# Attention scores in one float32r pass over stacked halves, maxima by pairs of rounds, weights four rounds behind

## The chip, the cores and the metric

The kernel runs on one core of a Trainium2 chip. The core has five engines that work side by side, each through its own list of instructions in order: PE (matrix products, with weight loads of its own shown as PEld), DVE (vector), ACT (activation functions), POOL (a second vector engine) and SP, which here only issues transfers (DMAs). PE writes to PSUM, a small memory of eight banks; the others read PSUM and the working memory, POOL the working memory only. The metric is the time on the device in microseconds (us); less is better.

## What is computed

Two layers. Each has a normalisation with a learned shift and scale, an attention and a feed-forward part. Only the attention of the first layer bears on the change: 16 batches of 256 tokens, 128 wide, 16 heads of 8.

```
qkv = x @ Wqkv + bqkv                  # q, k, v: 16 heads of 8
content = einsum('bhid,bhjd->bhij', q, k)
rel = einsum('bhid,rd->bhir', q, rel_emb)      # shifted by one, cut to 256
scores = (content + rel) / sqrt(8)
out = einsum('bhij,bhjd->bhid', softmax(scores), v) @ Wout + bout
```

`rel` is added to k beforehand, so that one product gives content and rel together. After that come a mixture of 16 experts (four chosen per token), then the second layer. All data are 32-bit floats.

## The kernel before

The work goes by chunks of two batches (8 chunks) and, in the attention of the first layer, by rounds: a round `n` is a batch `b` and a quarter `r` of its heads, so four heads, and there are 64 rounds, 8 per chunk. The 128 partitions hold four groups `g` of 32 rows. The main loop (over `n`, line 727 on) writes the order of every engine by hand; the scheduler keeps it. In each turn it issues:

- `scores(n)`: eight matmuls of 32 rows by 256 columns, two for each of four heads, each head in its own PSUM bank (`s`, L441). The operands are `qx` and `kx`: a head's 8 rows of q (others are zero, by the mask `of_head`), and k with a row of ones (row 16 of each group).
- `row_maxima` (L453): DVE takes the maximum over each row of `s`, negated. `with_maxima` (L461 to L465): DVE transposes the maxima, and SP writes them by four small DMAs into row 16 of `qx`, opposite the ones of k, so that the next product has the maximum subtracted.
- `weights(n - LAG)` with LAG = 2: the same product turned round, keys in rows (`st`, L475), and ACT's exp of it (L483).
- `values(n - LAG - 1)` (L495): the product with v, which ACT copies out (L506, L509) and POOL adds (L510).
- steps of other tasks, generators that stop at places ("dve", "mid", "end", "take", "after", "late"), of which one step per place is taken in a round: `project` (normalisation of the next chunk, `pq`, `pk`, `pv`: L568, L576, L590), `attn_end` (division, output product, gate), `chunk_end` (second normalisation, router logits, router).
- one of `later_loads`: DMAs of inputs that are needed later.

`projected` makes the operands: for each of NU = 2 halves of the heads it takes `pq` and `pk`, ACT writes `qx` from `pq` twice (L571), and DVE writes `kx` from `pk`, with the bias and `rel` added (L578). All PSUM tiles of the stage come from one pool of eight banks, `pa_m`; a bank goes to the next tile when the last reader of its old tile is through, and that next tile's first matmul waits for it. At the start ACT loads its table (L163) and applies tanh to the conditioning input (L163, `silu`); `project_first` then does chunk 0 batch by batch (L608 on).

Of the kernel before, what the change touches and what calls it, by code (L numbers as in the profile page):

```python
# [15 lines left out]
ENG = mybir.EngineType  # L16
IN_ORDER = {ENG.PE, ENG.DVE, ENG.Activation, ENG.Pool}

# [11 lines left out]
ONES = 16  # L30
# [26 lines left out]
def tile_adaln_two_layers(ctx: ExitStack, tc: tile.TileContext, a: dict, out: bass.AP):  # L57
# [53 lines left out]
    wq = load("wq", [P, NU, P], a["wq"])  # L111
    wk = load("wk", [P, NU, P], a["wk"])
    wv = load("wv", [P, P], a["wv"])
    bq = load("bq", [P, NR], a["bq"])
    of_head = load("of_head", [P, NS], a["of_head"])
    bk = load("bk", [P, NU], a["bk"])
# [147 lines left out]
    with ExitStack() as moe_scope:  # L264
# [87 lines left out]
        with ExitStack() as scope:  # L352
            ap = scope.enter_context(tc.tile_pool(name="attn", bufs=2))
            ap1 = scope.enter_context(tc.tile_pool(name="attn1", bufs=1))
            rt = scope.enter_context(tc.tile_pool(name="route", bufs=2))
# [14 lines left out]
            maxima = [ap1.tile([P, NIT, 32], F32, tag=f"maxima{i}", name=f"maxima{i}") for i in range(3)]  # L370

# [17 lines left out]
            for t in maxima:  # L389
                nc.gpsimd.memset(t, 0.0)  # L390
            filled(0, nc.vector)
# [38 lines left out]
            LAG = 2  # L430
# [3 lines left out]
            def scores(n):  # L434
# [3 lines left out]
                for i in range(NIT):  # L438
                    for g in range(4):
                        rows_ = slice(32 * g, 32 * g + 32)  # L440
                        nc.tensor.matmul(  # L441
                            s[g][:, i, :],
                            qs[c][r][rows_, k, ts(i, P)],
                            ks[c][rows_, r // NS, k, :],
                            start=True,
                            stop=True,
                        )
                return s

            def row_maxima(n, s):  # L450
                mx = maxima[n % 3]
                for g in range(4):
                    nc.vector.tensor_reduce(mx[:, :, g], s[g], AX.X, ALU.max, negate=True)  # L453
                return mx

            def with_maxima(n, mx):

                b, r = rounds[n]
                c, k = divmod(b, 2)
                turned = ap.tile([P, NIT, 32], F32, tag="turned", name=f"turned_{n}", bufs=3)  # L460
                nc.vector.transpose(turned.rearrange("p i t -> p (i t)"), mx.rearrange("p i t -> p (i t)"))  # L461
                row = qs[c][r].rearrange("(g x) k t -> x g k t", x=32)[ONES, :, k, :]
                row = row.rearrange("g (i m t) -> m g i t", i=NIT, m=4)
                for m in range(4):
                    nc.sync.dma_start(row[m], turned[32 * m : 32 * m + 4])  # L465

            def weights(n):
# [3 lines left out]
                st = [bank([P, NIT, T], f"st_{n}_{g}") for g in range(4)]  # L471
                for i in range(NIT):
                    for g in range(4):
# [3 lines left out]
                            ks[c][rows_, r // NS, k, ts(i, P)],  # L477
                            qs[c][r][rows_, k, :],
                            start=True,
                            stop=True,  # L480
# [73 lines left out]
            def operands(c):  # L554
                qs[c] = {r: ap.tile([P, 2, T], F32, tag=f"qx{r}", name=f"qx_{c}_{r}") for r in range(NR)}
                ks[c] = ap.tile([P, NU, 2, T], F32, tag="kx", name=f"kx_{c}")

            def projected(c, hT, of):
# [4 lines left out]
                for u in range(NU):  # L563
                    yield "mid"
                    if u == 0 and c:
                        operands(c)
                    pq = bank([P, n, T], f"pq_{at}_{u}")
                    nc.tensor.matmul(pq, wq[:, u, :], h2, start=True, stop=True)  # L568
                    for s in range(NS):
                        r = NS * u + s  # L570
                        nc.scalar.activation(  # L571
                            qs[c][r][:, of, :], pq, AF.Identity, bias=bq[:, r : r + 1], scale=of_head[:, s : s + 1]
                        )
                    yield "end"
                    pk = bank([P, n, T], f"pk_{at}_{u}")
                    nc.tensor.matmul(pk, wk[:, u, :], h2, start=True, stop=True)  # L576
                    yield "take"
                    nc.vector.scalar_tensor_tensor(  # L578
                        ks[c][:, u, of, :],
                        pk,  # L580
                        bk[:, u : u + 1],
                        rel.unsqueeze(1).to_broadcast([P, n, T]),
                        ALU.add,
                        ALU.add,
                    )
# [7 lines left out]
            def project(c):  # L593
# [4 lines left out]
                hT = ap.tile([P, 2, T], F32, tag="hT", name=f"hT_{c}")  # L598
# [113 lines left out]
            hT_first = ap.tile([P, 2, T], F32, tag="hT", name="hT_0")  # L712
# [13 lines left out]
            next_chunks = {max(LAG, 2 * NR * c): c + 1 for c in range(NCH - 1)}  # L726
            for n in range(len(rounds) + LAG + 1):
                if n < len(rounds):
# [5 lines left out]
                    with_maxima(n, row_maxima(n, s))  # L734
# [9 lines left out]
                take_step("end")  # L744
                take_step("take", True)
# [15 lines left out]
                if n == 40:  # L761

                    nc.gpsimd.tensor_scalar(b_gu[:, 0, :], b_gu[:, 0, :], ALPHA, None, ALU.mult)
                    nc.gpsimd.tensor_scalar(b_gu[:, 1, :], b_gu[:, 1, :], 1.0, None, ALU.add)
            take_step("take", True)

# [810 lines left out]
def _layout(inputs):  # L1577
# [6 lines left out]
    def at_heads(v):  # L1584

        o = np.zeros(v.shape[:-1] + (NU, 4, 32), f)
        v = v.reshape(v.shape[:-1] + (NU, NS, 4, DH))
# [74 lines left out]
```

## Time and profile before

| what | value |
| --- | --- |
| median of 3 runs | 1073.02 us (1072.72 to 1073.31) |
| the profiled run's own time | 1072.42 us |
| its span, first to last instruction | 1070.3 us |
| mean granted clock of PE | 0.993 |
| instructions | 15978 |
| first and last `s` of the attention rounds | 11.6 and 290 us |
| first matmul of the experts (L813) | 302.7 us |

A row of the page's groups names the line, the engine, the operation and the tiles (out<-in), how often it ran, its busy time, the mean duration in ns, and the idle time of its engine just before it with what ended that idle time. In the timelines the first two numbers are start and duration in us, x4 says that four instructions of one kind are merged into a row, and the bracket names the idle time of that engine before it and who ended it. In the table by stages each engine has its busy time and number of instructions, then come the clock of PE, the busy share of the DMA engines and GB/s. "SPq" rows are the issues of DMAs by SP.

### The profile page before, as it was taken

How to read it: one execution, taken by the hardware profiler on the slowest of the kernel's cores; microseconds unless marked ns; L12 is line 12 of the kernel's file. 1: busy time of each engine (PE TensorE's matmuls, PEld its weight loads, DVE VectorE, ACT ScalarE, POOL GpSimd, SP SyncE). 2: the span in 40 equal slices, each digit the busy share in tenths (PEclk: the TensorE clock that was granted, in tenths of full speed). 3: DMA queues.
4: the chain of work that ended last, by engine and by line, in shares of the span. 5: the costliest groups of instructions: out<-in, count | busy, mean ns of one | idle time of the engine just before them, and what ended most of it. 6: DMA issues, size and time to landing. Idle time of an engine off the chain costs nothing. (4 is left out here: it accounts for less than half of the span.)

```text
span 1070.3 us, 15978 instructions
## 1 busy us (share of the span) xinstructions
PE 1019.3 (95%) x5333; PEld 520.1 (49%) x5333; DVE 833.5 (78%) x1285; ACT 718.4 (67%) x1515; POOL 796.5 (74%) x756
## 2 busy tenths in 40 slices
PE   7999999999999999999999999898999999999987
PEld 5566666666654444444444434333444444444334
DVE  6678878998834466766656566899999999999995
ACT  3676677667666777687767756365676767767662
POOL 3245434543457678887888788899999999999992
PEclk8999999999999999999999999999999999999999
DMA  4102100000052222322222222100001000000000
GB/s 118 42 11 61 53 13 2 3 4 2 4 179 81 98 99 80 118 105 94 109 90 90 89 95 102 59 10 10 21 0 30 15 15 30 1 10 6 5 11 20
DMA packets 35537, 53.14 MB, mean 50 GB/s; under 512 B 8416, under 2 KB 23296, under 8 KB 35456
## 3 DMA queue, kind: packets, MB, share of 16 engines
q1 hardware_dynamic: 34912, 51.87, 14.5%
q8 instruction: 42, 0.69, 0.3%
q14 instruction: 39, 0.32, 0.1%
q10 hardware_dynamic: 544, 0.26, 0.1%
HBM read 46.34 MB, written 5.51 MB: 48 GB/s over the span
## 5 line engine op out<-in xcount | busy, mean ns | idle before, releaser
L483 ACT ACTIVATE exp<-st 128x512 f32<-128x512 f32 x256 | 132.2, 602 | 87.6 <-PE st L475 87.6
L453 DVE TENSOR_REDUCE maxima<-s 128x2 f32<-128x512 f32 x256 | 158.8, 683 | 26.2 <-PE s L441 26.0
L828 POOL TENSOR_TENSOR u<-u,wide 128x512 f32<-128x512 f32 x128 | 163.0, 1273 | 10.3 <-DVE u L827 0.2
L827 DVE SCALAR_TENSOR_TENSOR u<-pg,u 128x512 f32<-128x512 f32 x128 | 87.7, 686 | 78.8 <-POOL u L821 78.8
L836 PE MATMUL acc<-u,w_dn 128*128 128x512 f32 x256 | 134.0, 605 | 6.4 <-POOL u L828 6.2
L1241 DVE TENSOR_TENSOR_SCAN sum_assoc<-keep,bound_assoc 128x1024 f32<-128x1024 bf16 (+1 forms) x58 | 125.7, 2168 | 9.6 <-POOL bound_assoc L1238 9.6
L813 PE MATMUL pg<-hT,w_gu 128*128 128x512 f32 x256 | 131.2, 594 | 0.4 <-DVE logits L675 0.4
L815 PE MATMUL pup<-hT,w_gu 128*128 128x512 f32 x256 | 130.8, 593 | 0.6 <-ACT u L818 0.6
L821 POOL TENSOR_SCALAR u<-u 128x512 f32<-128x512 f32 x128 | 79.6, 622 | 62.8 <-ACT u L818 56.5
L1238 POOL TENSOR_TENSOR bound_assoc<-v,phasor 128x1024 f32<-128x1024 f32 x57 | 124.6, 2185 | 1.6 <-ACT phasor L1224 1.6
L1459 POOL TENSOR_TENSOR sum_assoc<-sum_assoc,phasor 128x1024 f32<-128x1024 f32 (+1 forms) x58 | 121.3, 2091 | 0.4 <-DVE sum_assoc L1241 0.3
L816 ACT ACTIVATE pg<-pg,b_gu 128x512 f32<-128x512 f32 x128 | 84.0, 656 | 52.6 <-PE pg L813 52.0
L1241 DVE TENSOR_TENSOR_SCAN mem<-keep,bound_pos 128x1024 f32<-128x1024 bf16 x52 | 118.1, 2271 | 0.0
L1238 POOL TENSOR_TENSOR bound_pos<-v,rotor 128x1024 f32<-128x1024 f32 x51 | 111.4, 2185 | 0.0
L1255 PE MATMUL pout<-m_pos,w_pos 128*128 128x512 f32 x204 | 97.2, 599 | 14.2 <-ACT oT L1280 10.8
L1255 PE MATMUL pout<-sum_assoc,w_assoc 128*128 128x512 f32 x228 | 107.6, 594 | 2.0 <-POOL sum_assoc L1459 2.0
L818 ACT ACTIVATE u<-pup,b_gu 128x512 f32<-128x512 f32 x128 | 87.8, 686 | 18.4 <-PE pup L815 16.4
L475 PE MATMUL st<-qx,kx 32*128 32x256 f32 x1024 | 82.6, 390 | 0.7 <-DMA qx<-turned 0.5
L836 PEld LDWEIGHTS acc<-u,w_dn 128*128 128x128 f32 x256 | 46.8, 190 | 73.9 <-issue 38.9
L441 PE MATMUL s<-kx,qx 32*128 32x256 f32 x1024 | 78.2, 407 | 4.1 <-DVE kx L578 1.8
L1222 ACT ACTIVATE phasor<-off 128x512 f32<-128x512 f32 x56 | 35.1, 627 | 69.6 <-DVE off L1216 64.2
L815 PEld LDWEIGHTS pup<-hT,w_gu 128*128 128x128 f32 x256 | 50.2, 196 | 60.5 <-issue 51.6
(302 smaller groups left out, 1866.8 us busy)
## 6 DMA issues: line engine op xcount, KB each, us to landing
wide<-scores SPq DMA_DIRECT2D x64, 512.0 KB
qx<-turned SPq DMA_DIRECT2D x256, 1.0 KB
there<-total SPq DMA_DIRECT2D x12, 256.0 KB
fetched<-there SPq DMA_DIRECT2D x12, 256.0 KB
w_gu<-in_gate_up_dram SPq DMA_DIRECT2D x8, 256.0 KB
out_dram<-x SPq DMA_DIRECT2D x16, 128.0 KB
x<-in_x_dram SPq DMA_DIRECT2D x14, 128.0 KB
w_dn<-in_down_dram SPq DMA_DIRECT2D x4, 256.0 KB
```

The source lines that it names most:

```text
L453: nc.vector.tensor_reduce(mx[:, :, g], s[g], AX.X, ALU.max, negate=True)
L483: nc.scalar.activation(e[:, g, :, :], st[g], AF.Exp, scale=QSCALE)
L813: nc.tensor.matmul(pg, w_gu[:, e, 0 : 2 * D : 2], h2, start=True, stop=True)
L815: nc.tensor.matmul(pu, w_gu[:, e, 1 : 2 * D : 2], h2, start=True, stop=True)
L818: nc.scalar.activation(u, pu, AF.Identity, bias=b_gu[:, 1, e : e + 1])
L827: nc.vector.scalar_tensor_tensor(u, pg, MOST, u, ALU.min, ALU.mult)
L828: nc.gpsimd.tensor_tensor(u, u, wide[n // SOME][:, n % SOME, :], ALU.mult)
L836: nc.tensor.matmul(accs[c], w_dn[:, e, :], work.pop(n), start=False, stop=(e == NE - 1))
L1238: nc.gpsimd.tensor_tensor(w[nm], v2, bind, ALU.mult)
L1241: nc.vector.tensor_tensor_scan(dst[:, half].rearrange("p s k t -> p (s k t)"), keep.rearrange("p (s k) t -> p s k t", k=2)[:, half].rearra ...
L1255: nc.tensor.matmul(pos[c], w[:, j, :], m[:, k, :, :].rearrange("p k t -> p (k t)"), start=(j == 0 and i == 0 and k == 0), stop=(c < NCH - ...
L1459: nc.gpsimd.tensor_tensor(m[:, part], m[:, part], phasor[(n - 1) % 3][:, part, :, 1:], ALU.mult)
```

## The change

- q and k are projected once each (128 rows, 16 heads of 8), not twice, and split in an upper half (the upper 20 bits, by an `and` on DVE) and the exact rest (a subtraction on POOL; for the k of chunk 0 on DVE). Both halves of both are stored to DRAM, each row twice, and read back by round, so that the 32 rows of a group hold the 8 rows of a head four times: upper and lower of q against upper and lower of k. The matmuls of `s` and `st` then run on type float32r.
- The stores and reads are queued in `copies` and issued 2 or 3 (6 before round 8) per round by SP; those of chunk 0 are issued at once, q's by ACT.
- The negated maxima of two rounds go into one tile `raw`, are split in the same way into 16 columns of `maxima`, are transposed once for two rounds, and go to 16 rows of a tile of their own, `max_rows`, by four DMAs. `with_maxima` of a pair stands behind the first reduction of the next even round.
- `weights` starts with four new matmuls of 512 columns (`takes` against `max_rows`), which add the maxima of the round to `st`. `takes` is made at the start by ACT from the input `of_round`.
- LAG is 4. The task that projects chunk 1 starts at round 1. The tiles of hT and of the router have one buffer less.

The diff, cut to its core:

```diff
-    wq = load("wq", [P, NU, P], a["wq"])
-    wk = load("wk", [P, NU, P], a["wk"])
+    wq = load("wq", [P, P], a["wq"])
+    wk = load("wk", [P, P], a["wk"])
...
-    bq = load("bq", [P, NR], a["bq"])
-    of_head = load("of_head", [P, NS], a["of_head"])
+    bq = load("bq", [P, 1], a["bq"])
+    of_round = load("of_round", [P, 2], a["of_round"])
...
+            for t in max_rows:
+                nc.gpsimd.memset(t.bitcast(F32), 0.0)
+            for i in range(2):
+                nc.scalar.activation(takes[:, i, :], ident, AF.Identity, bias=of_round[:, i : i + 1], scale=0.0)
             filled(0, nc.vector)
             sc0 = silu(0, cT0, setup)
...
-            LAG = 2
+            LAG = 4
...
-                            qs[c][r][rows_, k, ts(i, P)],
-                            ks[c][rows_, r // NS, k, :],
+                            qs[c][rows_, r, k, ts(i, P)],
+                            ks[c][rows_, r, k, :],
...
+            def upper(out, src):
+                nc.vector.tensor_scalar(out.bitcast(I32), src.bitcast(I32), UPPER_HALF, None, ALU.bitwise_and)
...
             def row_maxima(n, s):
-                mx = maxima[n % 3]
+                if n % 2 == 0:
+                    raws[n // 2] = small.tile([P, NIT, 4, 2], F32, tag="raw", name=f"raw_{n // 2}")
+                raw = raws[n // 2]
                 for g in range(4):
-                    nc.vector.tensor_reduce(mx[:, :, g], s[g], AX.X, ALU.max, negate=True)
+                    nc.vector.tensor_reduce(raw[:, :, g, n % 2], s[g], AX.X, ALU.max, negate=True)
+                    if g == 0 and n >= 2 and n % 2 == 0:
+                        with_maxima(n // 2 - 1)
+                if n % 2:
+                    mx = maxima[n // 2 % 3][:, :, 0:16].rearrange("p i (g h x) -> h p i g x", g=4, h=2)
+                    upper(mx[0], raw)
+                    nc.gpsimd.tensor_tensor(mx[1], raw, mx[0], ALU.subtract)
...
+                rows_ = max_rows[pair % 3].bitcast(F32).rearrange("(q x) (i m t) -> x m q i t", x=8, i=NIT, m=4)[0]
                 for m in range(4):
-                    nc.sync.dma_start(row[m], turned[32 * m : 32 * m + 4])
+                    nc.sync.dma_start(rows_[m], turned[32 * m : 32 * m + 16])
...
             def weights(n):
...
+                for g in range(4):
+                    rows_ = slice(32 * g, 32 * g + 32)
+                    nc.tensor.matmul(
+                        st[g],
+                        takes[rows_, n % 2, :],
+                        max_rows[n // 2 % 3][rows_, :].unsqueeze(1).to_broadcast([32, NIT, T]),
+                        start=True,
+                        stop=False,
+                    )
...
+            def halves(of_q, whole, engine):
...
+                upper(high, whole)
+                engine.tensor_tensor(whole, whole, high, ALU.subtract)
+                return high, whole
+
+            def put_aside(at, of_q, parts):
...
+                there = dram.tile([P, 4, n, T], F32, tag=f"{nm}_halves{n}", name=f"{nm}_halves_{at}")
+                to = there.rearrange("p (y z) k t -> z p y (k t)" if of_q else "p (y z) k t -> y p z (k t)", y=2)
+                return there, [
+                    (to[i], parts[i].rearrange("p k t -> p (k t)").unsqueeze(1).to_broadcast([P, 2, n * T]))
+                    for i in range(2)
+                ]
+
+            def spread(c, of, of_q, there, r, queue=nc.sync):
+
+                dst = (qs if of_q else ks)[c].bitcast(F32)[:, r, of, :]
+                queue.dma_start(dst, there[32 * r : 32 * r + 32].rearrange("n x k t -> (n x) k t"))
...
             def projected(c, hT, of):
...
+                pq = bank([P, n, T], f"pq_{at}")
+                nc.tensor.matmul(pq, wq, h2, start=True, stop=True)
+                qf = ap1.tile([P, 2, T], F32, tag="q_whole", name=f"q_whole_{at}")[:, 0:n, :]
+                nc.scalar.activation(qf, pq, AF.Identity, bias=bq)
+                q = halves(True, qf, nc.gpsimd)
+                yield "end"
+                pk = bank([P, n, T], f"pk_{at}")
+                nc.tensor.matmul(pk, wk, h2, start=True, stop=True)
+                yield "take"
...
+                k = halves(False, kf, nc.gpsimd if c else nc.vector)
+                both = []
+                for of_q, parts in ((True, q), (False, k)):
+                    queue = nc.scalar if of_q and not c else nc.sync
+                    there, moves = put_aside(at, of_q, parts)
+                    both.append((of_q, there, queue))
+                    copies.extend((lambda move=move, queue=queue: queue.dma_start(*move)) for move in moves)
+                copies.extend(
+                    (lambda r=r, each=each: spread(c, of, *each[:2], r, each[2])) for r in range(NR) for each in both
+                )
+                if not c:
+                    while copies:
+                        copies.pop(0)()
...
-            next_chunks = {max(LAG, 2 * NR * c): c + 1 for c in range(NCH - 1)}
+            next_chunks = {max(1, 2 * NR * c): c + 1 for c in range(NCH - 1)}
...
-                    with_maxima(n, row_maxima(n, s))
+                    row_maxima(n, s)
+                elif n == len(rounds):
+                    with_maxima(n // 2 - 1)
...
                 take_step("end")
+                for i in range(2 + n % 2 if n >= 2 * NR else 6):
+                    if copies:
+                        copies.pop(0)()
                 take_step("take", True)
```

## The prediction, made before the changed kernel ran

> **What bounds the kernel now.** I read the page first, then the DVE and PE timelines of the attention stage. All times are us.
>
> ```profile
> PE 1019.3 (95%) x5333; PEld 520.1 (49%) x5333; DVE 833.5 (78%) x1285; ACT 718.4 (67%) x1515; POOL 796.5 (74%) x756
> L453 DVE TENSOR_REDUCE maxima<-s 128x2 f32<-128x512 f32 x256 | 158.8, 683 | 26.2 <-PE s L441 26.0
> L475 PE MATMUL st<-qx,kx 32*128 32x256 f32 x1024 | 82.6, 390 | 0.7 <-DMA qx<-turned 0.5
> L441 PE MATMUL s<-kx,qx 32*128 32x256 f32 x1024 | 78.2, 407 | 4.1 <-DVE kx L578 1.8
> ```
>
> The change lies in the 64 rounds of attention. `s` (L441) and `st` (L475) run from 11.6 to about 298; what follows, 302.7 to the end, keeps its code, so it shifts as a whole. PE is busy almost always there, but a share of busy time does not say who waits for whom. The timelines do:
>
> ```profile
> 96.07 0.24 DVE L461 STREAM_TRANSPOSE turned<-maxima 128x64 f32<-128x64 f32 x1
> 96.86 2.48 DVE L453 TENSOR_REDUCE maxima<-s 128x2 f32<-128x512 f32 x4 [0.54 <-PE s L441]
> 101.20 2.48 DVE L453 TENSOR_REDUCE maxima<-s 128x2 f32<-128x512 f32 x4
> 289.56 1.15 PE L441 MATMUL s<-kx,qx 32*128 32x256 f32 x16
> 290.72 2.49 DVE L453 TENSOR_REDUCE maxima<-s 128x2 f32<-128x512 f32 x4 [0.75 <-PE s L441]
> ```
>
> The round at 96.86 has nothing on DVE but four reductions and a transposition: DVE idled 0.54 before it, PE sets the pace. The round at 101.20 followed two statistics, a reciprocal and a product on DVE and shows no idle: DVE sets the pace. So both engines are near their limit. Rounds take 3.3 to 5.2; from `s` of round 8 (49.1) to `s` of round 63 (289.56) they take 240.4, mean 4.37. DVE is busy some 203 of these (from the table by stages). **A faster PE can win at most what DVE leaves idle, about 37.**
>
> **PE, part by part.** A f32 matmul leaves two records (1024 records, 512 matmuls each for `s` and `st`); 16 records of `s` take 1.15, the last one 0.374 of it, so they follow at 52 ns. If a float32r matmul leaves one, `s` has 8 (0.42) and `st` 8 plus 4 new ones for the maxima (0.62), where each has 16 (0.83). From the start of `s` to DVE's first reduction it is 1.16 now (289.56 to 290.72); 8 records fewer take off 0.42, a record of half the passes some 0.1 (512 columns last 0.592, 256 last 0.374: 0.22 for 256 columns in two passes): 0.65 to 0.7. One `pq` and one `pk` per chunk go, 0.86 each (two records of 0.43). No row shows float32r: the ends are one record, as above, and two as now, with `s` to DVE at 1.16; I take one, the nearest row halved, since the diff asks for one pass.
> The Trainium skill, "TensorE: Matmul & The Clock Gate", section "LDWEIGHTS (loading the stationary operand)", says that a weight load costs its columns over 1.2 GHz, 32 rows or 128, so 107 ns here; by it the 12 loads of `st` would take 1.28, longer than now, PE would gain nothing, and the sum would be near the third rival's. This trace differs: 16 loads of `st`, each 0.185 long, pass in 0.85, so they follow at 44 ns; the measurement decides.
>
> **DVE, part by part.** Per chunk (8 rounds) it loses 4 of 8 transpositions (0.245 each) and one `kx` (0.75). It gains two masks of 128x512 (`q_high`, `k_high`) and four of 128x16. A mask of 128x512 from SBUF has no row; 128x256 (L1566) takes 0.34, the two-step 128x512 (L896) 0.84; I take 0.6. The small ones: 0.15 (128x16, L149 to L151, 0.16 to 0.28). Lost 1.7, gained 1.8: DVE's sum stays 29.4 per chunk, 32 x 0.62 of it reductions. POOL's new differences (1.27 each, row L828) lie beside reductions.
>
> A round is then 2.48 of reductions, 0.24 in even rounds, and the larger of DVE's other work and the hand-over: the banks of `s` free with the last reduction of the round before, so 0.7. The built order gives DVE's other work for a middle chunk: y and statistics 1.25; mask, statistics, inv, heads 1.75; none; mask, statistics, y 1.4; statistics and q/k halves, where `q_high` waits for ACT (four exp 2.06, po copy 0.40, q 0.80 behind one another) 3.4; mask, inv, heads 0.95; none; logits. Rounds: 3.95, 4.2, 3.4, 3.85, 6.1, 3.4, 3.4, 3.25: **31.55 per chunk**, against 33.5 (84.61 to 118.12) and later 35.2, the router's steps included. Those add 12 of DVE work, some 8.5 of it not hidden in light rounds. The last chunk has no q/k and no statistics for a next one (-3.9). Rounds 8 to 63: 7 x 31.55 - 3.25 (up to the `s` of 63) - 3.9 + 8.5 = 222.2, a gain of 18.2, **if the operands are there**.
>
> At nothing I cost: the transposition's new wait for POOL's small difference (0.2 to 0.7; it starts a reduction and a hand-over, 1.3, earlier; behind it on DVE three reductions; uncovered 0.5 every second round, 14); one buffer for hT and the router's tiles (readers were eight rounds, or one instruction of the same engine, ahead; uncovered 0.4 each); three q evictions fewer on ACT (0.8 each), which is not the limit.
>
> **The operands go through memory.** q and k halves are stored (512 KB each) and read back by round (256 KB). Prices: a 256 KB read issued alone at 903.92:
>
> ```profile
> 904.50:905.00 0.50, 0.50 (x2) 0.19 (x1) 0.50 (x1) 0.08 (x1) 0.50 (x1) 1.00 0.14 45
> 905.00:905.50 0.50, 0.50 (x3) 0.25 (x2) 0.50 (x2) 0.00 (x0) 0.50 (x1) 1.00 0.85 295
> 905.50:906.00 0.50, 0.50 (x3) 0.26 (x2) 0.50 (x2) 0.00 (x0) 0.50 (x1) 1.00 0.48 180
> 906.00:906.50 0.50, 0.50 (x3) 0.25 (x2) 0.50 (x2) 0.33 (x1) 0.50 (x2) 1.00 0.01 4
> 293.55 2.31 SPq L465 DMA_DIRECT2D qx<-turned  x4
> ```
>
> It lands 2.1 after its issue at some 320 GB/s; 512 KB so takes 2.85. Four small ones take SP 2.3.
> In SP's order the second store of k stands behind the four transfers of maxima of round 6 of the chunk, which wait for the transposition after that round's first reduction (1.6 after its `s`). Then: maxima issued by 3.9, store lands 6.65, first read of k (SP waits for the store) lands 8.6 to 9.0. `s` of the next chunk wants it after two rounds, 6.65. **PE stands 2.0 to 2.4, six times: 13.5**, and DVE with it; queued behind that `s` are all weights and values. What bounds it: nothing (if it lands in time) and 4 each (if reads of w_gu come between).
> The Trainium skill, "DMA: Bandwidth & Descriptors", section "Anatomy of one DMA — SWDGE (gpsimd) path", fits DMAs that GpSimd issues by 2.0 plus bytes over 436 GB/s: 2.6 and 3.2 for these two. By it a trip would be 0.85 longer, and the sum 5 longer; the trace has 2.1 for 256 KB from SP, and I keep that.
> Rounds 8 to 63 so take 222.2 + 13.5 = 235.7: a gain of 4.7.
>
> **The start.**
>
> ```profile
> 1.75 1.28 ACT L163 ACT_TABLE_LOAD   x1 [1.75 <-issue]
> 3.46 0.29 DVE L608 BATCH_NORM_STATS2 stats_a<-x 128x6 f32<-128x128 f32 x1
> 4.01 0.44 SPq L71 DMA_DIRECT2D of_head<-in_of_head_dram  x1
> 11.56 1.15 PE L441 MATMUL s<-kx,qx 32*128 32x256 f32 x16
> ```
>
> ACT's table load and silu now stand behind two `takes`, which wait for `of_round`, in of_head's place on SP (4.01), behind transfers that keep the DMA engines full until 5.5: about 6.1. Then 1.28, two takes 0.6, silu 0.2, DVE 0.3: DVE's statistics begin at 8.5, not 3.46, and all to `pq` moves by **5.0**. Then, where `s` followed `kx`: q (0.56), mask, difference, store of 256 KB, read of 128 KB; 1 MB of stores passes at 320 GB/s, so k's last lands near 20, its read near 22. `s` of round 0 at 22.0: **+10.4** in all.
> Rounds 0 to 3 carry no weights and are short, but batch 1 needs its own trip: 18.4 to round 4, now 19.1 (30.70 - 11.56): -0.7. Chunk 1's four stores (2 MB, 6.4) go out together after round 6's maxima; its first read of k lands about 13.5 after `s` of round 6, where 6.7 was wanted: rounds 4 to 8 take 24.1, now 18.4: **+5.7**. At round 8 the kernel is 15.4 late.
>
> **The end.** Four rounds of weights behind instead of two: two more rounds with neither `s` nor DVE work, each bound by exp and PE's `st`, `po` in turn. Now such a round is 3.05 (po at 294.99, 298.04); st is 0.2 shorter: **+5.7**.
>
> **Sum.** 15.4 - 4.7 + 5.7 = +16.4. The profiled run took 1072.4 (span 1070.3 and 2.1 around it; the median of the runs shown is 1073.0, 0.6 more): 1088.8, so 1089.0.
>
> **Rivals.**
> 1. The trip through memory is short (store and read together about 3, not 5). For: DMA is nearly idle in this stage (share 0.02 to 0.16 between 100 and 250), and the read is mostly a fixed wait. Then the six stands go (-13.5), chunk 1's shrinks by 4, the two first trips by 2 each: 1067.5, faster. It decides from 2.1 less per trip on, nine trips making up 17 to 19. Against: 256 KB alone took 2.1, and a store must land before its read is issued. Chance 0.2 for ending faster.
> 2. The trip is longer: stores slower than reads, maxima queued behind 512 KB, each stand 4: 1089 + 11 = 1100, with slower first trips 1104. Chance 0.15.
> 3. float32r does not do what it says (two records per matmul): hand-over 1.2, four light rounds per chunk lose 0.5: 1089 + 14 = 1103. Chance 0.07.
> 4. The trip is in time in the middle but not at the start: 1075, about the same. Chance 0.08.
>
> **The numbers.** My case (1080 to 1098) has 0.5. 0.2% (2 us) is about what a measurement of this kernel can tell from no change. Faster 0.2, same 0.05, slower 0.75. The range from 1068 to 1104 takes in rivals 1 and 2 for the most part.
>
> **What will show it.** Right: first `s` near 22; `s` and `st` with 512 and 768 records; DVE waits of 2 or more before the first reduction of each chunk from the second on; rounds 26 and 30 of a chunk near 3.4; MoE start near 319. Wrong: `s` of round 16, 24 and so on right behind the round before; stage end before 303; a hand-over under 0.5; a DVE mask over 0.8.

## The result and the profile after

The changed kernel takes 1117.17 us (four runs, 1116.04 to 1117.6); the kernel before, on the same chip, 1073.07. The ratio is 1.041 (95% interval 1.0397 to 1.0424). Predicted were 1089 and, as range, 1068 to 1104. The direction was right; the loss is 44, not 16.4, and the time lies outside the range.

From the page of the changed kernel: the line of the engines, then the groups of `s`, of its reduction and of ACT's exp.

```profile
PE 987.4 (89%) x4529; PEld 482.2 (43%) x4529; DVE 836.2 (75%) x1296; ACT 703.6 (63%) x1490; POOL 823.9 (74%) x807
L468 DVE TENSOR_REDUCE raw<-s 128x2 f32<-128x512 f32 x256 | 160.4, 677 | 57.7 <-PE s L448 57.5
L448 PE MATMUL s<-kx,qx 32*128 32x256 f32 x512 | 43.2, 381 | 52.1 <-DMA kx<-k_halves 39.8
```

`s` has 512 records where it had 1024: float32r leaves one record per matmul. But PE, busy nearly all the time before, now idles 52 ahead of `s` (below, a stand is such a time in which PE waits for an operand), 40 of it until a read of `kx` lands, and DVE idles 57.5 for `s`, where it was 26.

The table gives the span in five stretches, with borders read from the timelines (first reduction of a round on DVE, first expert matmul on PE). "Predicted" is the profile before plus the prediction's terms. Two experiments are shown beside it.

| stretch | before | predicted | after | `early` | `spaced` |
| --- | --- | --- | --- | --- | --- |
| to round 0 | 12.8 | 23.2 | 24.2 | 24.5 | 21.7 |
| rounds 0 to 8 | 37.5 | 42.5 | 49.5 | 50.0 | 34.2 |
| rounds 8 to 63 | 240.5 | 235.8 | 254.4 | 227.9 | 226.8 |
| round 63 to the experts | 12.0 | 17.7 | 17.3 | 17.6 | 18.5 |
| experts to the end | 767.6 | 767.6 | 770.2 | 767.3 | 768.2 |
| span | 1070.3 | 1086.8 | 1115.5 | 1087.4 | 1069.4 |

So 28.7 were missed: 18.6 in rounds 8 to 63, 7 in rounds 0 to 8, 2.6 after the stage and 1 ahead of it, less 0.4 at its end. Rounds 8 to 63 are where the gain was to be, and there the kernel loses 14.

What a chunk's border looks like, from the timeline of the changed kernel between 101 and 113 (start, duration, engine; SPq is SP issuing transfers; rows of other work left out):

```profile
101.55 0.23 DVE L479 STREAM_TRANSPOSE turned<-maxima 128x64 f32<-128x64 f32 x1
101.84 2.57 SPq L484 DMA_DIRECT2D max_rows<-turned  x4
...
104.51 0.53 SPq L638 DMA_DIRECT2D k_halves<-k_whole  x1
105.14 0.41 SPq L609 DMA_DIRECT2D qx<-q_halves  x1
105.60 0.84 SPq L272 DMA_DIRECT2D w_gu<-in_gate_up_dram  x1
...
107.83 0.32 SPq L609 DMA_DIRECT2D kx<-k_halves  x1
...
111.27 0.80 PE L448 MATMUL s<-kx,qx 32*128 32x256 f32 x8 [4.38 <-DMA kx<-k_halves]
```

This is the chain the prediction described, one link after the other (below, a trip is a store to memory and the read back). The maxima of rounds 12 and 13 are turned in round 14; their four transfers occupy SP until 104.41; only then k's second store goes out. SP waits for its landing (3.3) before it issues the read at 107.83, and that needs 3.4. PE had nothing to do from 106.9.

The landing times are in the page's part on transfers (KB each, median us from issue to landing):

```profile
qx<-q_halves SPq DMA_DIRECT2D x28, 256.0 KB, 3.2
kx<-k_halves SPq DMA_DIRECT2D x28, 256.0 KB, 3.6
q_halves<-q_whole SPq DMA_DIRECT2D x7, 512.0 KB, 3.2
k_halves<-k_high SPq DMA_DIRECT2D x7, 512.0 KB, 4.0
k_halves<-k_whole SPq DMA_DIRECT2D x7, 512.0 KB, 3.2
```

The last row is k's second store. The prediction had 2.1 for a read and 2.85 for a store.

### The profile page after: what moved, and what is told of

Read it like the earlier page. It is cut to its first block, busy times and chain, and to the rows that moved or that the text cites. A ratio compares the mean times of both kernels' runs of the same rounds, so it can differ in the third digit from the quotient of the medians.

```text
span 1115.5 us, 14249 instructions
## 1 busy us (share of the span) xinstructions
PE 987.4 (89%) x4529; PEld 482.2 (43%) x4529; DVE 836.2 (75%) x1296; ACT 703.6 (63%) x1490; POOL 823.9 (74%) x807
## 5 line engine op out<-in xcount | busy, mean ns | idle before, releaser
L468 DVE TENSOR_REDUCE raw<-s 128x2 f32<-128x512 f32 x256 | 160.4, 677 | 57.7 <-PE s L448 57.5
L1321 PE MATMUL pout<-m_pos,w_pos 128*128 128x512 f32 x204 | 99.7, 612 | 12.5 <-ACT oT L1346 9.9
L884 ACT ACTIVATE u<-pup,b_gu 128x512 f32<-128x512 f32 x128 | 87.8, 686 | 18.2 <-PE pup L881 16.2
L448 PE MATMUL s<-kx,qx 32*128 32x256 f32 x512 | 43.2, 381 | 52.1 <-DMA kx<-k_halves 39.8
L523 PE MATMUL po<-exp,v_aug 128*32 128x256 f32 x1024 | 79.9, 432 | 9.2 <-DVE raw L468 9.0
```

Source lines behind the costliest of these rows:

```text
L468: nc.vector.tensor_reduce(raw[:, :, g, n % 2], s[g], AX.X, ALU.max, negate=True)
L884: nc.scalar.activation(u, pu, AF.Identity, bias=b_gu[:, 1, e : e + 1])
L1321: nc.tensor.matmul(pos[c], w[:, j, :], m[:, k, :, :].rearrange("p k t -> p (k t)"), start=(j == 0 and i == 0 and k == 0), stop=(c < NCH - ...
```

## The experiments

**Theory A**: the loss is waiting in SP's one queue (stores behind maxima, reads behind stores, maxima behind reads) and in two trips one behind the other at the start; float32r and the light rounds bring what was expected. **Rival B**: the load on the DMA engines, PE's granted clock after a stand, or DVE's new work cost the time, wherever the transfers are put. **Rival C**: a new order only moves the wait from the reads to the maxima.

| run | median (range) | ratio to before, 95% |
| --- | --- | --- |
| changed kernel | 1117.2 (1116.0 to 1117.6) | 1.0397 to 1.0424 |
| `late_takes` | 1110.7 (1110.0 to 1112.0) | 1.0344 to 1.0378 |
| `six_copies` | 1106.5 (1103.6 to 1109.8) | 1.0296 to 1.0346 |
| `stale` | 1112.8 (1110.8 to 1117.2) | 1.0360 to 1.0409 |
| `direct` | 1152.1 (1149.8 to 1153.6) | 1.0727 to 1.0760 |
| `same_round` | 1112.8 (1109.5 to 1117.2) | 1.0349 to 1.0408 |
| `q_on_dve` | 1116.4 (1114.8 to 1117.6) | 1.0393 to 1.0424 |
| `three` | 1105.0 (1104.7 to 1108.3) | 1.0294 to 1.0327 |
| `three_two_pass` | 1138.3 (1137.1 to 1139.2) | 1.0597 to 1.0632 |
| `early` | 1089.1 (1087.8 to 1090.3) | 1.0138 to 1.0168 |
| `early_all` | 1083.7 (1080.6 to 1085.3) | 1.0078 to 1.0121 |
| `early_zero` | 1084.1 (1080.6 to 1085.1) | 1.0080 to 1.0122 |
| `filler` | 1114.8 (1112.5 to 1119.0) | 1.0365 to 1.0406 |
| `in_first_wait` | 1072.3 (1070.1 to 1078.4) | 0.9992 to 1.0023 |
| `first_straight` | 1085.9 (1082.8 to 1087.4) | 1.0104 to 1.0136 |
| `spaced` | 1070.1 (1064.9 to 1072.9) | 0.9957 to 0.9987 |
| `spaced_two_pass` | 1119.2 (1118.3 to 1119.4) | 1.0424 to 1.0452 |

### The takes moved: late_takes

```diff
-            for i in range(2):
-                nc.scalar.activation(takes[:, i, :], ident, AF.Identity, bias=of_round[:, i : i + 1], scale=0.0)
             filled(0, nc.vector)
...
             start(project_first(1, hT_first), rank=0)
+            for i in range(2):
+                nc.scalar.activation(takes[:, i, :], ident, AF.Identity, bias=of_round[:, i : i + 1], scale=0.0)
```

> The two takes on ACT come after the work of the first batch instead of ahead of the table load and silu; nothing else changes. Theory A (the start waits for ACT behind of_round: table load at 6.33, silu at 8.23 in the changed kernel, 1.75 and 3.1 before): everything up to the first pq moves 4 to 5 earlier, first reduction at 19 to 20 instead of 24.19, total 1112 to 1113. Rival (the first modulation waits for wmod or x, or the batch for wq, so that silu is not what is late): first reduction within 1 of 24.19, total 1116 to 1118.

Measured: first reduction at 18.83 instead of 24.19, 6.4 less in all. ACT's table load is back at 1.76. In the changed kernel it began at 6.33, when `of_round` had landed: two instructions that wait for this input, ahead of the table load, cost 5.4 up to the first reduction, as the prediction had it (5.0).

### The order on SP changed: six_copies, same_round

```diff
# six_copies
-                for i in range(2 + n % 2 if n >= 2 * NR else 6):
+                for i in range(6):
```

> SP takes six stores and reads of the halves per round in all chunks (the changed kernel: two or three from round 16 on), so k's second store and the first reads no longer stand behind the maxima's four transfers. Theory A (the stand before each chunk's first scores is the order of SP's queue): the last rounds of chunks 2 to 6, now 7.4 to 9.2, fall to 3.2 to 4.5, 18 to 25 less in all, total 1092 to 1100. Rival B (landing under load sets it, the transfers are just slow together): they fall by under 1 each, total 1112 to 1118. Rival C (the maxima now come late behind reads that wait for their stores, so weights wait): the stand goes but a new one of 2 to 4 per chunk comes with max_rows as its releaser, total 1105 to 1115.

```diff
# same_round
-                for i in range(2 + n % 2 if n >= 2 * NR else 6):
-                    if copies:
-                        copies.pop(0)()
                 take_step("take", True)
+                for i in range(4):
+                    if copies:
+                        copies.pop(0)()
```

> SP takes up to four of the copies after the round's take, so the four stores of a chunk are issued in the round that makes the halves, ahead of the next maxima, and the reads one and two rounds later, when the stores have landed; nothing else changes. Theory A (the stands are SP's order: k's second store behind the maxima's four transfers, the read behind that store): rounds 15, 23, 31, 39, 47, 55 fall from 7.4 to 9.2 to 3.1 to 3.7, round 7 from 11.57 to 4 to 6, first rounds of a chunk stay at 3.4 to 5.4; total 1083 to 1089. Rival C (as with six copies per round: a read that waits for its store holds up the maxima, and st waits for max_rows instead): a new stand of 2 to 3 per chunk, total 1095 to 1103. Rival B (DMA load): total 1108 or more.

By its total `six_copies` (1106.5) lies in C's range, above A's. `same_round` (1112.8) lies above C's range and in the one that B gave; what it shows in the trace is C's stand, only dearer. In `six_copies` the last rounds of chunks 1 to 6 fall from 47.5 to 29.5 in sum, but the first rounds of chunks 2 to 7 rise from 25.7 to 35.7. The timeline of `six_copies` shows why, around its round 24:

```profile
133.28 0.83 SPq L638 DMA_DIRECT2D k_halves<-k_whole  x1
...
133.95 0.23 DVE L479 STREAM_TRANSPOSE turned<-maxima 128x64 f32<-128x64 f32 x1
135.25 0.33 SPq L609 DMA_DIRECT2D qx<-q_halves  x1
...
138.19 0.33 SPq L609 DMA_DIRECT2D kx<-k_halves  x1
138.57 1.25 SPq L272 DMA_DIRECT2D w_gu<-in_gate_up_dram  x1
139.91 2.57 SPq L484 DMA_DIRECT2D max_rows<-turned  x4
...
143.77 0.80 PE L493 MATMUL st<-max_rows,takes 32*128 32x512 f32 x4 [2.08 <-DMA max_rows<-turned]
```

The maxima were turned at 133.95, but SP sat in reads that wait for stores and issued them 6 later than that; now `st` waits for `max_rows`. `same_round` shows the same (turned at 132.45, issued at 139.81, `st` idle 2.29), and its first rounds of chunks 3 to 7 take 6.5 to 8.6. Reordering this queue, in which most entries wait for something, traded most of one stand for another; 10.7 and 4.4 were gained.

### The wait for the store taken out, the DMAs left: stale

```diff
+                seen.append([there for _, there, _ in both])
                 copies.extend(
-                    (lambda r=r, each=each: spread(c, of, *each[:2], r, each[2])) for r in range(NR) for each in both
+                    (lambda r=r, i=i, each=each: spread(c, of, each[0], seen[-2][i] if c > 1 else each[1], r, each[2]))
+                    for r in range(NR)
+                    for i, each in enumerate(both)
                 )
```

> From chunk 2 on the reads fetch the halves of the chunk before, which were stored eight rounds earlier; stores and reads stay in number and place (the output so uses q and k of another chunk). What goes is the wait for the store alone; the read keeps its 3.5 from issue to landing. Theory A (store, then read, one behind the other): the first read of k is issued 3.1 earlier, so each of the stands of 4 to 6 shrinks by 3 to 3.3, 16 to 20 in all, total 1097 to 1101. Rival B (load on the DMA engines, or PE's granted clock, or DVE's rounds): total 1112 to 1118.

Measured: 4.4 less, far from the 16 to 20 expected; Theory A in this narrow form (the wait for the store) fell, and the total lies in Rival B's range. In the trace the first k read of a chunk goes out 0.9 to 2.9 after k's store instead of 3.2 to 4.1, but now shares the DMA engines with it and lands after 2.9 to 5.5 instead of 2.6 to 3.4. So here the load on the DMA engines took back much of what the wait had cost. The rest of the stand would be when SP gets to the store at all, behind the maxima; slack should cure both, and two rounds of it are tried below.

### Without memory in between: direct

```diff
+            def spread(c, of, of_q, part, x, r, queue):
+                dst = (qs if of_q else ks)[c].bitcast(F32)[:, r, of, :].rearrange("(p x) k t -> x p k t", x=4)[x]
+                queue.dma_start(dst, part[32 * r : 32 * r + 32])
```

> The halves go from SBUF to their rows in one transfer, without a store and a read of memory: 32 transfers of 64 KB per chunk instead of 4 of 512 KB and 8 of 256 KB. Theory A (two trips one behind the other are what is late, at the start as at each chunk): first reduction 2 to 4 earlier than 24.19, batch 1 and chunk 1 each 3 to 6 earlier, the last rounds of the chunks at 3.2 to 4 instead of 7.4 to 9.2; total 1070 to 1085. Rival (SP's issues are the limit: 32 at about 0.45 are 14 per chunk, and the maxima's transfers wait behind them): the maxima become the releaser of st, total 1095 to 1110.

(Here SP also takes up to eight copies per round.) Measured: 35 slower, far outside both ranges; of the two, the rival named the cause that the trace shows, at too low a price. The first reduction is 2.9 earlier and the last rounds of chunks 1 to 6 are down to 3.3 to 5.4, but SP issues 32 transfers per chunk, and between 60 and 300 PE stands 20.2 before `s` for `kx` and 12.8 before `st` for the maxima. SP's timeline in `direct`:

```profile
118.51 0.59 SPq L598 DMA_DIRECT2D qx<-q_whole  x1
119.15 0.59 SPq L598 DMA_DIRECT2D qx<-q_high  x1
119.79 0.59 SPq L598 DMA_DIRECT2D qx<-q_whole  x1
120.42 1.23 SPq L598 DMA_DIRECT2D kx<-k_high  x2
```

Each issue costs SP 0.59 to 0.64, so 32 take some 19 of a chunk's 41 to 46.

### Three places at once: q_on_dve, three, three_two_pass

```diff
-                q = halves(True, qf, nc.gpsimd)
+                q = halves(True, qf, nc.gpsimd if c else nc.vector)
```

> The difference of q's halves of chunk 0 is made by DVE (0.42, as k's is) instead of POOL, where that of batch 1 stood behind the memset of v_aug, the constants and chunk 1's normalization (33.95 to 39.66). Theory A: the store of q's lower half goes 3 to 4 earlier, s of round 4 with it: round 3 falls from 10.0 to 6 to 7, total 1112.5 to 1114. Rival (the stand at round 4 is two trips through memory whatever POOL does): round 3 over 9, total 1116 to 1118.

> The three edits together: takes late, the copies in the round that makes them, chunk 0's q difference on DVE. If they are independent places on one path, the gains add: 6.4 measured for the takes, 28 to 34 and 3 to 4 expected for the others: 1073 to 1080, about the time of the kernel before. What is then left against it: the first trip (s of round 0 some 7 later than before), the rounds of batch 1, and 5 at the end. Rival (the places hide one another, another stand takes over): 1085 to 1095.

> The same three edits, but with the operands of s and st as plain float32 (the halves stacked as they are, every matmul in two passes): what float32r alone is worth once the operands are there. Theory A (s to DVE 0.65 instead of 1.2 decides the light rounds, 4 to 5 per chunk, 0.5 each): 14 to 20 slower than the run with the three edits. Rival (DVE and ACT set the rounds, PE has slack): within 4 of it.

`q_on_dve`: round 3 falls from 10.0 to 8.24, less than expected, and the total by 0.8, within the interval; POOL was a small part of that stand. `three`: 1105, neither the 1073 to 1080 of its theory nor the rival's 1085 to 1095; another stand took over, as the rival had it, but a larger one: the first rounds of chunks 3 to 7 have grown to 6.3 to 8.6 as in `same_round`. `three_two_pass` differs from `three` by `F32R = mybir.dt.float32` alone and is 33 slower, more than either side expected. Each matmul of `s` and `st` then leaves two records instead of one (called two passes here), and PE becomes the bound (busy 199.6 of the 200 from 100 to 300, against 160.0 in `three`).

### Two rounds of slack: early, early_all, early_zero

After these, Theory A was narrowed to A': SP is one queue in which everything waits for something, so that no order helps, only slack.

```diff
-            next_chunks = {max(1, 2 * NR * c): c + 1 for c in range(NCH - 1)}
+            next_chunks = {max(1, 2 * NR * c - 2): c + 1 for c in range(NCH - 1)}
...
+                if c not in qs:
+                    operands(c)
                 dst = (qs if of_q else ks)[c].bitcast(F32)[:, r, of, :]
...
+                for i in range(2 if c else 0):
+                    yield "after"
                 yield "mid"
                 tiles = slice(2 * of.start, 2 * of.stop)
```

> The projection of chunks 2 to 7 starts two rounds earlier (the operand buffers are taken when the first read is issued, v is copied at its old place), so a chunk's stores leave SP two rounds earlier and its reads find them landed; order and number of transfers per round stay. Theory A' (SP is one queue in which stores wait for POOL's differences, reads for stores, and maxima for both, so that only slack helps): rounds 15, 23, 31, 39, 47, 55 fall to 3.1 to 4, the first rounds of a chunk stay at 3.4 to 5.4, no max_rows stand; total 1086 to 1092. Rival (the steps of the projection now fall on rounds that were full, on DVE or ACT, or a transfer is late elsewhere): 1095 to 1108. Chunk 1 is as in the changed kernel, its stand of 8 stays.

Measured: 1089.1, 28 less, as Theory A' had it. The number of bytes, of transfers and their landing times (3.3 to 3.6 for the reads) are as in the changed kernel; only the projection, and with it the stores, comes two rounds earlier. So it is not the load of the DMA engines by itself. Two things differ from what was expected. The last rounds of chunks 1 to 6 take 3.0 to 4.8, not 3.1 to 4. And a stand before `st` for `max_rows` came after all: 2.66 in round 10, which takes 9.5 (its cause is given with `spaced` below). PE's granted clock rises with the stands gone, from 0.91 to 0.93 in the mean over rounds 8 to 63, so part of the 28 may be the clock's. The timeline of `early` at its round 24 (its `s` is at 137.70, with no idle time in brackets):

```profile
129.19 0.53 SPq L638 DMA_DIRECT2D k_halves<-k_whole  x1
...
132.48 0.33 SPq L611 DMA_DIRECT2D kx<-k_halves  x1
...
137.70 0.54 PE L448 MATMUL s<-kx,qx 32*128 32x256 f32 x6
```

The same trip, now with 2 to spare. Chunks 2 and 3 take 31.47 and 32.2; the prediction had 31.55 without stands.

> early, with the takes late and chunk 0's q difference on DVE. If they add (6.4 measured for the takes, 2 in the profile for the difference): 7 to 9 faster than early, 1078 to 1085.

> early_all, with chunk 1's projection begun in round 0 instead of 1, so that part of it falls into PE's stand before round 4. Theory A': rounds 4 to 8 of the changed kernel take 26.7 (before 18.4) because chunk 1's stores stand behind the maxima of round 6; one round earlier they go out ahead of them: 4 to 8 faster than early_all, 1072 to 1079. Rival (batch 1's projection now stands behind chunk 1's on POOL or PE): same as early_all or up to 4 slower.

`early_all` gained 5.3 against `early` (7 to 9 expected). `early_zero` (as the first line of the diff, with 0 for 1) gained nothing on `early_all`, as its rival had it: chunk 1's `pq` still came in round 5, and its stores still stood behind the maxima of round 6.

### PE kept busy in the stand: filler

```diff
+                    if n and n % (2 * NR) == 0:
+                        fill = bank([P, 512], f"fill_{n}")
+                        for i in range(4):
+                            nc.tensor.matmul(fill, ident, wmod0[:, 0:512], start=True, stop=True)
                     s = scores(n)
```

> The changed kernel, with four matmuls of 128x512 (3.4 at full clock, their result is not used) on PE ahead of the first scores of chunks 1 to 7, where PE stands 4 to 9. Rival B (a stand also costs through the granted clock: 0.5 for 3.4 to 6.8 after it, a po then takes 1.93 instead of 1.07): clock in these stretches near 1, each chunk 0.5 to 1 shorter, 4 to 7 in all, total 1110 to 1113. Theory A (the stands alone; after one DVE sets the round): within 2 of the changed kernel.

Inconclusive: 1114.8, with an interval that overlaps the changed kernel's, and the clock was not kept at 1 everywhere (0.5 for 13.7 from 254 on). In the two profiles the first two rounds of chunks 2 to 7 take 52.1 in sum against 54.1, so 2 is an estimate of what the clock costs there; its whole share of the 44 is not shown.

### The start: in_first_wait, first_straight, spaced

`in_first_wait` is `early_zero` with batch 1 projected inside the wait for batch 0's trip:

```diff
-            for place in ("mid", "mid", "end", "take", "mid"):
-                take_step(place)
+            take_step("mid")
             start(project_first(1, hT_first), rank=0)
+            for place in ("dve", "mid", "end", "take", "mid", "mid", "mid", "end", "take", "mid"):
+                take_step(place)
...
-                for i in range(2 * k):
-                    yield "after"
                 yield "mid"
                 pt = bank([P, NIT, P], f"pln_a0_{k}")
```

> early_zero, with batch 1 projected in the 6.6 that PE, DVE and ACT wait for batch 0's trip (its halves in tiles of their own region), the reads of chunk 0 all on SP, so that ACT is not held up by a store; chunk 1's projection then falls into rounds 2 and 3. Theory (the start's lateness is the chain of two trips per batch and chunk, each begun only after the scores ahead of it): rounds 0 to 4 take 16 to 18 (21.8 in early_zero), rounds 4 to 8 take 14 to 19 (26.7), first reduction of round 8 at 53 to 57 instead of 68; total 1068 to 1074, as fast as the kernel before or faster. Rival (the DMA engines at the start, share 0.45 to 0.5, are the limit, or SP's issues): round 8 at 61 or later, total over 1077.

Measured: 1072.3, the time of the kernel before. Round 8 begins at 53.9 instead of 68.2: the start's lateness was the chain of trips. Its first round then takes 11.5, for a reason the run was not made for:

```profile
47.76 0.23 DVE L477 STREAM_TRANSPOSE turned<-maxima 128x64 f32<-128x64 f32 x1
49.31 0.33 SPq L616 DMA_DIRECT2D kx<-k_halves  x1
...
55.25 3.77 SPq L482 DMA_DIRECT2D max_rows<-turned  x4
...
61.50 0.80 PE L491 MATMUL st<-max_rows,takes 32*128 32x512 f32 x4 [8.00 <-DMA max_rows<-turned]
```

It is `six_copies` again: with six copies per round before round 16, SP ran ahead into the reads and let the maxima lie for 7.3; then, behind those reads, the first of them took 5.5 to land.

> in_first_wait, with batch 0's halves sent from SBUF to their rows directly (32 transfers of 32 KB, the first four of q on ACT's queue, the rest on SP). Theory (of the first trip the store is 3.3): first reduction of round 0 2 to 3 earlier than in in_first_wait, total 2 to 3 less. Rival (SP needs 0.45 to 0.58 for each of 28, some 14, and batch 1's stores stand behind them): round 4 as late as in early_zero or later, total 3 to 8 more than in_first_wait.

`first_straight` (batch 0 by 32 direct transfers): first reduction 1.7 earlier, the total 13.6 more than `in_first_wait` (the rival had 3 to 8). SP issues the 28 from 13.9 to 31.8, and round 4 begins at 41.3, as late as in `early_zero` (41.4), as the rival had it.

```diff
# spaced, against in_first_wait
-                for i in range(2 + n % 2 if n >= 2 * NR else 6):
+                for i in range(2 + n % 2):
```

> in_first_wait, but SP takes two or three copies per round from the start on, as it does from round 16 in the changed kernel, not six. In in_first_wait weights of round 4 stand 8.0 for max_rows: the maxima were turned at 47.7, but SP, which had run ahead into reads that wait for their stores, issued them at 55.25. Theory (SP's order again): the maxima leave at about 48, that stand goes, round 8 falls from 11.47 to 4 to 5, the first k read of chunk 1 is issued at 50 and lands at about 53.7, just in time: total 1064 to 1067, faster than both kernels. Rival (the reads now come late for rounds 8 to 11): 1068 to 1073.

> spaced, with plain float32 operands for s and st: what float32r is worth where neither the trip nor SP holds up the rounds. In the kernel before rounds 8 to 63 took 240.5; with float32r and slack they take 228. If a slower s costs its 0.5 only in light rounds (four per chunk): 14 more than spaced. If PE becomes the bound of most rounds, as the run three_two_pass suggests (33 more than three): 25 to 35 more.

`spaced` takes 1070.1: a ratio to the kernel before of 0.9972 (0.9957 to 0.9987), 0.3% faster than the kernel before, by less than the 1064 to 1067 expected. The first round of chunk 1 is down to 3.3, but round 10 takes 7.9, with PE idle 2.30 before `st` until `max_rows` lands. This stand is not SP's order. SP issued those four transfers from 56.80 on, right behind the load of `gates` (4 KB) at 55.91; that load landed only at 64.17, 8.3 after its issue, and the four landed just behind it, from 64.35 to 64.90. In `early` the same load (8.6 to land) makes the stand of round 10, and in the changed kernel one of 1.48 in the same round. `spaced_two_pass` is 49 slower, more than any theory had. The table by stretches (length, busy time and number of records of PE, PEld, DVE, ACT and POOL, then PE's granted clock, DMA share, GB/s), of `spaced_two_pass`:

```profile
100.00:150.00 50.00, 50.00 (x615) 35.52 (x608) 36.40 (x86) 28.43 (x63) 23.34 (x38) 1.00 0.45 135
```

and of `spaced`:

```profile
100.00:150.00 50.00, 45.11 (x552) 29.43 (x552) 44.70 (x101) 35.90 (x78) 29.76 (x46) 1.00 0.61 193
```

With two passes PE is busy without a gap, and DVE gets through 36 of work in 50; with one, both are busy 45, and more gets done. Stacked operands without float32r make PE the bound, at 40.1 per chunk (chunks 2 and 3).

## Why the prediction was right and wrong

**PE, right.** One record per matmul, 512 for `s` and 768 for `st`; rival 3 (two records) is out. From `s` to the first reduction it is 0.53 at full clock (86.62 to 87.15), 0.65 to 0.7 predicted.

**DVE, right.** Busy 836.2 in all against 833.5. The masks of 128x512 took 0.43 to 1.0 (0.6 predicted; over 0.8 had been named as a sign of being wrong, but the rounds do not show it), the light rounds 3.1 (3.25 to 3.4), the round with the halves 5.4 to 6.4 (6.1). Where nothing stands, a middle chunk takes 31.5 (`spaced`, chunks 2 and 3: 31.50 and 31.62); predicted were 31.55.

**The stands, the step that failed**: "PE stands 2.0 to 2.4, six times: 13.5". The mechanism was the one named, the size was not. Rounds 15, 23, 31, 39, 47 and 55 take 47.5 in sum; with a light round of 3.25 and stands of 2.25 they would take 33.0, so 14.5 were missed here. The stands so measured are 4.7 in the mean, above even the 4 each that the prediction gave as a bound. Two terms were too small, each by about 7.

- The price of the trip: over these six, k's second store lands after 3.3 and the first read after 2.8 in the mean (each read from the trace), 6.1 against 2.85 + 2.1, so 6 x 1.15 = 7. The 2.1 came from the one read that went out alone, and the store was scaled from it. (The Trainium skill, "DMA: Bandwidth & Descriptors", section "Anatomy of one DMA — SWDGE (gpsimd) path", whose fit is for DMAs that GpSimd issues and which the prediction weighed and set aside, gives 2.6 and 3.2; both prices came out nearer to that here.)
- When the store gets its turn on SP: the four small transfers were issued by 5.16 after `s` of round 6 of the chunk in the mean (4.3 to 6.0, read from the trace), not by 3.9, so 6 x 1.26 = 7.6. The transfers themselves occupied SP for 2.6 to 3.1, not 2.3, which is about half of it; the transposition was through 2.1 after that `s`, not 1.6; at chunk 3 a load of `w_gu` (0.87) stood ahead of them as well.

(Small slips of the prediction's working, which do not matter: 3.9 + 2.85 is 6.75, not 6.65; at 320 GB/s 512 KB would take 2.9, not 2.85; three rounds of the kernel before take 5.3, beyond its "3.3 to 5.2".) SP issues fewer transfers per chunk than before (28 for maxima and operands instead of 32); but the 12 new ones wait, for POOL, for stores, for one another, and what waited in this queue held up what stood behind it. The other 4.1 that rounds 8 to 63 missed lie outside these six rounds, about half of them in chunk 1, where the load of `gates` made a stand; the rest is open.

**The start, half wrong.** The takes (+5.0, measured 5.4) and `s` of round 0 (22.0, measured 23.4) were right. "Batch 1 needs its own trip: -0.7" was +3.7: rounds 0 to 4 take 22.8, because that trip begins only after round 2's reductions (begun earlier, in `in_first_wait`, these rounds take 16.5), and less so because POOL's difference stood behind a memset and a normalisation (33.95 to 39.66; on DVE, in `q_on_dve`, they take 21.7). Chunk 1's "+5.7" was +8.3; with the four stores under way together the last took 5.3 to land. At round 8 the kernel is 23.4 late, not 15.4.

**The end, right.** +5.3 for two more rounds of lag, +5.7 predicted.

**After the stage** 2.6 were lost where the prediction had a plain shift. Part of it is PE at half clock in the first 3.4 of the experts (a pair of `pg` records takes 1.68, later 1.02); the rest is open.

**Rivals.** Rival 1 (a short trip) was wrong from the price on. Rival 2 (a longer trip, stands of 4, 1100 to 1104) came nearest and named one of the two terms, the slower stores; it was 13 short, by some 8 in rounds 8 to 63, 4 at the start and 2 behind them. The fourth (in time in the middle) is what `early` makes true by other means.

**What the change would be worth**: float32r brings 33 to 49 here, against two passes over the same operands. Against the kernel before, which has fewer matmuls per round, the whole change gains 12.6 to 13.7 in rounds 8 to 63 once the operands are there in time (`early`, `spaced`), where 18.2 had been predicted for them without stands.

## What to carry to other kernels

A change that moves data through memory adds entries to an in-order queue, and the price of each is what is queued behind it while it waits: list the queue's entries in their order with what each waits for, before and after, and compare the time of a whole cycle with the time between two things that must be punctual. Here such a stand was cured by slack (the producer two rounds earlier: 28 gained), while reordering moved most of the wait to another entry (4.4 and 10.7 gained). Transfer prices should come from transfers issued in company, not from the one that had the engines to itself: here 2.1 alone, 2.6 to 3.4 in company.

## What the hardware showed unexpectedly

After the stands of rounds 15, 23, 31, 39, 47 and 55 PE ran at half its clock, in pieces that are multiples of 3.4. The table by stretches of the changed kernel, for the stand at round 16, what follows, and the time after:

```profile
106.90:111.20 4.30, 0.00 (x0) 0.00 (x0) 0.42 (x1) 0.67 (x2) 1.54 (x3) 0.89 0.97 276
111.20:117.00 5.80, 5.73 (x64) 3.75 (x68) 4.80 (x12) 2.86 (x7) 1.23 (x3) 0.50 0.29 94
117.00:124.00 7.00, 5.37 (x72) 3.12 (x65) 5.67 (x15) 4.41 (x11) 4.99 (x9) 1.00 0.64 217
```

The granted clock (third number from the end) is 0.50 for 5.8 after 4.3 without a matmul; the 16 records of `po` then take 1.93 instead of 1.07. The Trainium skill, "TensorE: Matmul & The Clock Gate", section "Part 1: The HAM clock gate (the "warmup" mystery)", says that an idle window of about 3.4 brings the halved clock and a busy one of that length ends it. This trace agrees in the lengths: the pieces of half clock up to the experts are 3.41, 6.83, 10.24 and 17.07 long. But PE need not have stood still for that long: the piece that begins at 233.1 has, in the 7 before it, no gap longer than 0.8 between matmuls.

The issues on SP with a source in SBUF cost more in these traces: 0.59 for `qx<-q_high` in `direct`, 0.43 for a read of `k_halves` in `early`. And several of the experiments scatter more than the kernel before: `spaced` 1064.9 to 1072.9, while the kernel before stayed within 1070.6 and 1074.7 (the changed kernel does not: 1116.0 to 1117.6); why is open.
